# A selective state-space block with FFN on one core: half of the scan inputs made by GpSimd, and what goes with it

## Chip, core and metric

The kernel runs on one core of a Trainium2 chip. The metric is the device time of one execution in microseconds; the time given for a kernel is the median of its runs.

## The reference

x has shape (2, 1024, 512). The block is a state-space layer with a residual and a layer norm, then an FFN with a residual and a layer norm, all in float32:

```python
xn = x * rsqrt(mean(x*x) + 1e-6) * norm_w
xn = xn * sigmoid((xn @ select_proj_w.T + select_proj_b) * select_gate)
delta, B, C = split(xn @ x_proj_w.T, 128 each)
dt = softplus(delta @ dt_proj_w.T + dt_proj_b)        # (2, 1024, 512)
A = -exp(A_log)                                       # (512, 128)
h[t] = exp(dt[t] * A) * h[t-1] + (dt[t] * xn[t]) * B[t]   # h: (2, 512, 128), 1024 steps
y[t] = sum_n h[t][:, n] * C[t][n]
x = layernorm(x + (y + x * D_param) @ out_proj_w.T)
x = layernorm(x + (silu(x @ w_gate.T) * (x @ w_up.T)) @ w_down.T)   # 512 -> 2048 -> 512
```

u stands below for dt * xn. The state h has 512 channels times 128 state indices for every token, and the recurrence runs along the tokens.

## The kernel before

The 2 x 1024 tokens are cut into 64 steps of 32 tokens (S = 32, NS = 64), the steps into two halves of 256 channels, and each half into 8 groups of 32 channels: 1024 groups, counted by k in the main loop. The 128 state indices lie on the partitions. One group is one VectorE instruction, a scan over 32 channels times 32 tokens, laid end to end in the free dimension (L694). Its factors, exp(dt A), come from a_sb, and its addends, u B, from the PSUM tile bu. The factor of each channel's first token is kept at 0 so that the channels do not run into one another; what the step before carries over goes into the first addend instead (L691).

Both inputs are outer products over (state, channel x token), and TensorE makes them with matmuls of 32 rows. For the decay, the weights are 32 rows of A_log and the moving tile ddt holds dt[c, t] on the diagonal (row c, channel c) and zero elsewhere; ScalarE takes the exponential out of PSUM into a_sb (decay_mm, decay_exp, L391 and L398). For B u, the weights are 32 tokens of B and the moving tile du holds u[t, c] where row and token agree (L678). GpSimd makes ddt and du by multiplying a row that is repeated with the mask hot (function diag, L362 and L372); u and B come through DRAM, from u_d and b_d, in function load.

y_round multiplies the finished half of h by C, four tokens at a time, with the columns of cz as weights (L410). y_out takes the result from PSUM and keeps in each row only the tokens that belong to it, by the mask pick and two additions on GpSimd (L424 to L426); post adds x * D, multiplies by the output projection and normalizes. pre makes dt, u, B and C for a chunk of 256 tokens (8 steps), ffn the FFN of a chunk.

The order of all this is written out by hand. Each turn of the loop over k issues: steps of the waiting pieces on other engines (work.others), the B u matmuls of group k and the decay matmuls of group k + 1, the exponentials, the scan of group k, then the y matmuls that ROUNDS gives this turn and as many pieces of pre, post and ffn (work.tensor) as PARTS allows. Every engine runs its own instructions in that order. All transfers go through SyncE's queue. carry_a and carry_h compute what a step hands to the next; pre of a chunk must be done by the last step of the chunk before.

Of the kernel before, what the change touches and what calls it, by code (L numbers as in the profile page):

```python
# [9 lines left out]
FP = mybir.dt.float32  # L10
# [10 lines left out]
ROUNDS = ((), (0, 1, 2), (), (), (3, 4, 5), (), (), (6, 7))  # L21
PARTS = (4, 0, 3, 3, 0, 3, 3, 0)
# [3 lines left out]
V_NORM, V_SELB, V_GATE, V_DTB = range(4)  # L26

# [7 lines left out]
def kernel(  # L35
# [9 lines left out]
    sel_t: bass.AP,  # L45
    xp_t: bass.AP,
# [32 lines left out]
    u_d = dram.tile([B * L, D], FP, name="u_d")  # L79
# [15 lines left out]
    pick = const.tile([P, 4], FP, name="pick")  # L95
    nc.gpsimd.tensor_copy(pick, hot[:, 0:4])
    for g in range(1, 8):
        nc.gpsimd.tensor_tensor(pick, pick, hot[:, ts(g, 4)], ALU.add)
# [9 lines left out]
    sel_w = main.tile([P, NM, D], FP, name="sel_w")  # L108
    xp_w = main.tile([P, NM, R + 2 * N], FP, name="xp_w")
    dt_w = main.tile([P, D], FP, name="dt_w")  # L110

    a_sb = main.tile([P, 3, 32, S], FP, name="a_sb")
# [18 lines left out]
    nc.sync.dma_start(sel_w, sel_t.rearrange("(k p) e -> p k e", p=P))  # L131
    nc.sync.dma_start(xp_w, xp_t.rearrange("(k p) e -> p k e", p=P))
# [5 lines left out]
    nc.gpsimd.memset(a_sb, 0.0)  # L138
    for t in cz:
        nc.gpsimd.memset(t, 0.0)  # L140
# [23 lines left out]
    def pre(c):  # L164
# [6 lines left out]
        rms = pre_pool.tile([P, TC], FP, tag="rms", name=f"rms_{c}")  # L171
        low = pre_pool.tile([P, TC], FP, tag="low", name=f"low_{c}")
        dt = pre_pool.tile([P, NM, TC], FP, tag="dt", name=f"dt_{c}", bufs=2)
        u = pre_pool.tile([P, NM, TC], FP, tag="u", name=f"u_{c}")
        c_sb = pre_pool.tile([P, TC], FP, tag="c_sb", name=f"c_sb_{c}", bufs=2)
        made[c] = dt, c_sb
        xn = xT

        def matmuls(ps, w, m, rhs):
            for k in range(NM):  # L180
                nc.tensor.matmul(  # L181
                    ps[:, 0:TC], w[:, k, ts(m, P)], rhs[:, k, :],
                    start=(k == 0), stop=(k == NM - 1),
                )
                yield "H" if k + 1 < NM else "E"
# [30 lines left out]
        for m in range(NM):  # L216
            ps = misc(f"sel_{c}_{m}")
            yield from matmuls(ps, sel_w, m, xn)
            nc.scalar.activation(
                u[:, m, :], ps[:, 0:TC], AF.Relu,  # L220
                bias=neg[:, 1, m : m + 1], scale=neg[:, 0, m : m + 1],
            )
            nc.scalar.activation(
                dt[:, m, :], ps[:, 0:TC], AF.Abs, bias=gate_b[:, m : m + 1], scale=col(V_GATE, m)
            )
            yield "P" if m + 1 < NM else "E"
# [9 lines left out]
        for g, dst in ((0, low), (2, c_sb)):  # L236
            ps = misc(f"xp_{c}_{g}")
            yield from matmuls(ps, xp_w, g, xn)
            nc.scalar.copy(dst, ps[:, 0:TC])
            yield "P"  # L240

        ps = misc(f"b_{c}")
        for j in range(NJ):
            for k in range(NM):
                nc.tensor.matmul(  # L245
                    ps[:, ts(j, N)], xn[:, k, ts(j, P)], xp_w[:, k, R : R + N],
# [3 lines left out]
        bt = pre_pool.tile([P, NJ, N], FP, tag="bt", name=f"bt_{c}")  # L250
        nc.scalar.copy(bt, ps[:, 0:TC].rearrange("p (j n) -> p j n", j=NJ))
# [19 lines left out]

        for j in range(NJ):
            yield "P"
            ps = misc(f"uT_{c}_{j}")
            for m in range(NM):
                nc.tensor.transpose(ps[:, ts(m, P)], u[:, m, ts(j, P)], ident)
                if m == 1:
                    yield "H"
            yield "E"
            t = pre_pool.tile([P, D], FP, tag="row", name=f"uT_{c}_{j}")  # L280
            nc.scalar.copy(t, ps)
            nc.sync.dma_start(u_d[c * TC + j * P : c * TC + (j + 1) * P, :], t)
            if c == 0 and j == 0:
                load(0)
                diag(0, 0)
                diag(0, 1)
# [26 lines left out]
    prepared, carried, dus, ddts, hs, ys = {}, {}, {}, {}, {}, {}  # L313

    def load(st):


        ub = step_pool.tile([P, 2, P], FP, tag="ub", name=f"ub_{st}")
        rows = u_d[ts(st, S), :].rearrange("t (m g c) -> g t m c", g=4, c=32)
        for g in range(4):  # L320
            nc.sync.dma_start(
                ub[ts(g, S), 0, :].rearrange("t (m c) -> t m c", c=32), rows[g]
            )
            nc.sync.dma_start(ub[ts(g, S), 1, :], b_d[ts(st, S), :])
        prepared[st] = ub
# [4 lines left out]
        if st % NSB:  # L330
            cd = step_pool.tile([P, D], FP, tag="cd", name=f"cd_{st}")
            nc.sync.dma_start(cd, dt0_d[st : st + 1, :].to_broadcast([P, D]))
            carried[st] = cd

    def carry_a(st):
# [3 lines left out]
        cd = carried[st]  # L339
        nc.gpsimd.tensor_tensor(cd, a_n, cd, ALU.mult)  # L340
        nc.scalar.activation(cd, cd, AF.Exp, scale=-1.0)

    def carry_h(st, i):

        if st % NSB == 0:
            return
        cd = carried[st].rearrange("p (b i e) -> p b i e", i=2, e=16)[:, :, i, :]
        last = hs[2 * (st - 1) + i][:, :, S - 1].rearrange("p (b e) -> p b e", e=16)
        nc.gpsimd.tensor_tensor(cd, cd, last, ALU.mult)  # L349

    def diag(j, part):

        h, a = j // 2, 2 * (j % 2)
# [3 lines left out]
        name, m = divmod(part, 2)  # L357
        shape = [P, 2, 16, S]
        if name == 0:
            if m == 0:  # L360
                ddts[j] = half_pool.tile(shape, FP, tag="ddt", name=f"ddt_{j}")
            nc.gpsimd.tensor_tensor(  # L362
                ddts[j][:, m, :, :],
                made[st // SPC][0][:, a + m, toks(st)].unsqueeze(1).to_broadcast([P, 16, S]),
                hot[:, ts(i, 16)].unsqueeze(2).to_broadcast([P, 16, S]),
                ALU.mult,
            )
        else:
            if m == 0:
                dus[j] = half_pool.tile(shape, FP, tag="du", name=f"du_{j}")  # L370
            uv = prepared[st][:, 0, :].rearrange("p (m i e) -> p m i e", i=2, e=16)[:, :, i, :]
            nc.gpsimd.tensor_tensor(  # L372
                dus[j][:, m, :, :],
                uv[:, a + m, :].unsqueeze(2).to_broadcast([P, 16, S]),
                hot.unsqueeze(1).to_broadcast([P, 16, S]),
                ALU.mult,
            )
# [8 lines left out]
    def decay_mm(k, b):  # L386
# [3 lines left out]
        ps = ps_a.tile([P, 16, S], FP, tag="a", name=f"a_{k}_{b}")  # L390
        nc.tensor.matmul(  # L391
            ps, a_t[ts(g, 32), m, :], ddts[k // 4][ts(g, 32), m % 2, :, :],
            start=True, stop=True,
        )
        return ps

    def decay_exp(k, b, ps):
        nc.scalar.activation(  # L398
            a_sb[:, k % 3, ts(b, 16), 1:], ps[:, :, 1:], AF.Exp, scale=-1.0
        )  # L400
# [16 lines left out]
    def y_out(st):  # L417

        tt, s = divmod(st, 4)
        if s == 0:  # L420
            yrs[tt] = post_pool.tile([P, 4, P], FP, tag="yr", name=f"yr_{tt}")
        yc = post_pool.tile([P, P, 4], FP, tag="yc", name=f"yc_{st}")
        nc.scalar.copy(yc, ys.pop(st).rearrange("p (q t) -> p q t", t=4))  # L423
        nc.gpsimd.tensor_tensor(yc, yc, pick.unsqueeze(1).to_broadcast([P, P, 4]), ALU.mult)  # L424
        nc.gpsimd.tensor_tensor(yc[:, :, 0:2], yc[:, :, 0:2], yc[:, :, 2:4], ALU.add)
        nc.gpsimd.tensor_tensor(yrs[tt][:, s, :], yc[:, :, 0], yc[:, :, 1], ALU.add)  # L426
        if s == 3:
            work.add(post(tt), front=True)

    yrs = {}  # L430

    def post(tt):

        zT = post_pool.tile([P, NM, P], FP, tag="zT", name=f"zT_{tt}")
        nc.sync.dma_start(zT, x_q.rearrange("(m p) t -> p m t", p=P)[:, :, ts(tt, P)])
        yield "E"
        yield "E"
        nc.gpsimd.tensor_tensor(zT, zT, dq.unsqueeze(2).to_broadcast([P, NM, P]), ALU.mult)
        yield "E"
        yield "P"  # L440
        ps = misc(f"zT_{tt}")
        for s in range(4):
            nc.tensor.transpose(ps[:, ts(s, P)], yrs[tt][:, s, :], ident)
            if s == 1:
                yield "H"
        yield "E"
        z = zT.rearrange("p m (s t) -> p s m t", t=S)
        nc.vector.tensor_tensor(
            z, z, ps.rearrange("p (s m t) -> p s m t", m=NM, t=S), ALU.add
        )  # L450
# [28 lines left out]
    def ffn(c):  # L479
# [13 lines left out]
        def fetch(n):  # L493
            while len(pieces) < min(n, len(sources)):
                i = len(pieces)
                pieces.append(
                    ffn_pool.tile([P, 2 * D], FP, tag="w", name=f"w_{c}_{i}", bufs=4)
# [18 lines left out]
        for what in order:  # L516
            part = int(what[1])
            if what[0] == "g":
                hid = hid_pool[0].tile([P, NH, TC], FP, tag="hid", name=f"hid_{c}_{part}")
                hids[part] = hid, []  # L520
                for f in range(NH):
# [14 lines left out]
                    work.add(silu(gu, hid[:, f, :], f"{c}_{part}_{f}", hids[part][1]), front=True)  # L536
# [4 lines left out]
            for half in range(2):  # L541
                fetch(at + 4)
                for j in range(NJ):
                    yield "P"
                    ps = misc(f"d_{c}_{part}_{half}_{j}")
                    for f in range(NH):
                        w = pieces[at + f // 4].rearrange("p (f d) -> p f d", f=4)
# [12 lines left out]
    def silu(gu, dst, name, ready):  # L560


        e = ffn_pool.tile([P, TC], FP, tag="e", name=f"e_{name}", bufs=2)
# [4 lines left out]
        nc.scalar.activation(e, g, AF.Exp, scale=-1.0)  # L568
        nc.scalar.activation(e, e, AF.Ln, bias=ones[:, 0:1])
        yield "E"  # L570
        nc.scalar.activation(e, e, AF.Exp, scale=-1.0)  # L571
# [231 lines left out]
```

## Time and profile before

| | us |
|---|---|
| median of 3 runs | 2905.64 (2905.34 to 2907.6) |
| profiled execution, its own time | 2913.85 |
| its span, first to last instruction | 2912.1 |
| first scan starts | 64.7 |
| last scan ends, about | 2790.4 |
| 1024 scans, busy | 2340.5 |

| engine | busy us | share of the span |
|---|---|---|
| TensorE | 2751.4 | 94% |
| VectorE | 2529.0 | 87% |
| ScalarE | 1560.2 | 54% |
| GpSimd | 1783.5 | 61% |

The granted TensorE clock is 0.978 in the mean; the DMA moves 154.58 MB, 53 GB/s. In the profile PE is TensorE, PEld its weight loads, DVE VectorE, ACT ScalarE, POOL GpSimd, SPq the transfers that SyncE issues; a line in a list of groups gives the source line, the engine, output <- inputs, shapes, count, busy time and mean duration, and behind the second bar the idle time ahead of these instructions with what ended it. A float32 matmul shows as two records.

### The profile page before, as it was taken

The page shows a single profiled execution, that of the slowest core. Times are in us where ns is not written, and L with a number is a line of the kernel's source. Part 1 is how long each engine was busy: PE and PEld are TensorE (multiplying, and loading weights), DVE is VectorE, ACT ScalarE, POOL GpSimd, SP SyncE. Part 2 cuts the span into 40 slices and gives each one's busy share as a digit, 9 for nine tenths or more (in the row PEclk, how much of TensorE's full clock was granted, in tenths as well). Part 3 has the DMA queues.
Part 4 walks back from the last instruction along what each step waited for, and adds up shares of the span by engine and source line. Part 5 has one row for each costly group of instructions (what it writes and reads, how often), then busy time and mean ns, then how long its engine had stood idle before and what let it go on. Part 6 is the DMA issues. An engine that isn't in the chain of part 4 may idle for free.

```text
span 2912.1 us, 53232 instructions
## 1 busy us (share of the span) xinstructions
PE 2751.4 (94%) x20608; PEld 1383.1 (47%) x20608; DVE 2529.0 (87%) x2176; ACT 1560.2 (54%) x3073; POOL 1783.5 (61%) x2006
## 2 busy tenths in 40 slices
PE   5988789999999999999999999999999999999989
PEld 3433234444444444444544444444444444444467
DVE  0899999999899999998899999999998999999930
ACT  3554446545565455654555556555565555454533
POOL 4564556757577576665656757666675666666633
PEclk7999999999999999999999999999999999999999
DMA  2000001212112120111211221121111112111223
GB/s 82 8 19 19 19 14 57 67 45 71 55 29 63 55 70 32 54 55 50 66 32 48 65 66 55 32 75 48 59 46 56 52 55 70 44 62 60 61 82 125
DMA packets 110170, 154.58 MB, mean 53 GB/s; under 512 B 46752, under 2 KB 69792, under 8 KB 109920
## 3 DMA queue, kind: packets, MB, share of 16 engines
q1 hardware_dynamic: 109920, 151.19, 17.1%
q8 instruction: 164, 2.69, 0.4%
q14 instruction: 86, 0.70, 0.1%
HBM read 141.57 MB, written 9.57 MB: 52 GB/s over the span
## 4 chain that ended last, share of the span: by engine, by line
PE 69%; DVE 22%; issue 3%; ACT 2%; POOL 2%; DMA 1%; DVEq 0%; SPq 0%; POOLq 0%; ACTq 0%
PE bu L678 25%; DVE h L694 19%; PE gu L529 16%; PE y L410 12%; PE d L548 5%; PE a L391 4%; PE op L457 2%; PE sel L181 2%; ACT a_sb L398 1%; DVE bu L691 1%; PE xp L181 1%; PE ss L195 1%; DMA u_d<-uT 1%; PE b L245 1%; POOL du L372 0%
## 5 line engine op out<-in xcount | busy, mean ns | idle before, releaser
L694 DVE TENSOR_TENSOR_SCAN h<-a_sb,bu 128x1024 f32<-128x1024 f32 x1024 | 2340.5, 2286 | 183.3 <-PE bu L678 66.1
L398 ACT ACTIVATE a_sb<-a 128x496 f32<-128x496 f32 x2048 | 1089.5, 585 | 1064.1 <-PE a L391 945.1
L678 PE MATMUL bu<-du,ub 32*128 32x512 f32 x4096 | 1216.7, 648 | 79.5 <-DVE h L694 45.7
L391 PE MATMUL a<-ddt,a_t 32*128 32x512 f32 x4096 | 1259.3, 650 | 10.7 <-ACT t L297 8.0
L362 POOL TENSOR_TENSOR ddt<-dt,hot 128x512 f32<-128x512 f32 x512 | 533.8, 1050 | 358.7 <-PE a L391 358.7
L678 PEld LDWEIGHTS bu<-du,ub 32*128 32x128 f32 x4096 | 344.2, 185 | 484.8 <-issue 287.6
L372 POOL TENSOR_TENSOR du<-ub,hot 128x512 f32<-128x512 f32 x512 | 536.1, 1052 | 57.3 <-PE a L391 47.8
L410 PE MATMUL y<-h,cz 128*32 128x256 f32 x8192 | 533.6, 390 | 2.4 <-DVE h L694 2.4
L529 PE MATMUL gu<-x1T,w 128*128 128x256 f32 x2048 | 519.0, 395 | 4.9 <-DMA w<-in_wgu_s_dram 3.4
L529 PEld LDWEIGHTS gu<-x1T,w 128*128 128x128 f32 x2048 | 368.3, 190 | 254.1 <-issue 180.5
L410 PEld LDWEIGHTS y<-h,cz 128*32 128x32 f32 x8192 | 230.5, 111 | 418.5 <-issue 308.6
L391 PEld LDWEIGHTS a<-ddt,a_t 32*128 32x128 f32 x4096 | 379.2, 185 | 42.1 <-ACT a_sb L398 27.4
L565 POOL TENSOR_SCALAR gu<-gu 128x256 f32<-128x256 f32 x128 | 108.5, 848 | 271.1 <-ACT gu L535 270.9
L548 PE MATMUL d<-w,hid 128*128 128x256 f32 x1024 | 256.9, 394 | 10.5 <-DVE x L554 8.2
L691 DVE TENSOR_TENSOR bu<-bu,cd 128x32 f32<-128x32 f32 x992 | 184.1, 186 | 87.8 <-PE a L391 80.5
L548 PEld LDWEIGHTS d<-w,hid 128*128 128x128 f32 x1024 | 185.0, 190 | 127.5 <-issue 82.3
L424 POOL TENSOR_TENSOR yc<-yc,pick 128x512 f32<-128x512 f32 x64 | 66.6, 1041 | 146.4 <-ACT yc L423 146.4
L349 POOL TENSOR_TENSOR cd<-cd,h 128x256 f32<-128x256 f32 x124 | 106.8, 862 | 60.4 <-DVE h L694 60.3
L572 POOL TENSOR_TENSOR hid<-gu,e 128x256 f32<-128x256 f32 x128 | 93.3, 729 | 74.6 <-ACT e L571 73.9
L554 DVE TENSOR_TENSOR x<-x,d 128x256 f32<-128x256 f32 x64 | 25.6, 399 | 101.7 <-PE d L548 101.7
L535 ACT COPY gu<-gu 128x512 f32<-128x512 f32 x128 | 75.3, 588 | 67.6 <-PE gu L529 67.4
L566 POOL TENSOR_TENSOR gu<-gu 128x256 f32<-128x256 f32 x128 | 94.3, 737 | 10.7
(86 smaller groups left out, 1258.8 us busy)
## 6 DMA issues: line engine op xcount, KB each, us to landing
w<-in_wgu_s_dram SPq DMA_DIRECT2D x128, 512.0 KB, 3.7
w<-in_wd_s_dram SPq DMA_DIRECT2D x64, 512.0 KB, 3.6
cd<-dt_d SPq DMA_DIRECT2D x62, 256.0 KB, 3.7
xT<-in_x_t_dram SPq DMA_DIRECT2D x8, 512.0 KB, 4.7
u_d<-uT SPq DMA_DIRECT2D x16, 256.0 KB, 2.0
ub<-u_d SPq DMA_DIRECT2D x256, 16.0 KB, 2.0
ub<-b_d SPq DMA_DIRECT2D x256, 16.0 KB, 1.9
zT<-in_x_q_dram SPq DMA_DIRECT2D x16, 256.0 KB, 4.4
```

Of the source, the lines that this page charges most:

```text
L349: nc.gpsimd.tensor_tensor(cd, cd, last, ALU.mult)
L362: nc.gpsimd.tensor_tensor(ddts[j][:, m, :, :], made[st // SPC][0][:, a + m, toks(st)].unsqueeze(1).to_broadcast([P, 16, S]), hot[:, ts(i, ...
L372: nc.gpsimd.tensor_tensor(dus[j][:, m, :, :], uv[:, a + m, :].unsqueeze(2).to_broadcast([P, 16, S]), hot.unsqueeze(1).to_broadcast([P, 16, ...
L391: nc.tensor.matmul(ps, a_t[ts(g, 32), m, :], ddts[k // 4][ts(g, 32), m % 2, :, :], start=True, stop=True,)
L398: nc.scalar.activation(a_sb[:, k % 3, ts(b, 16), 1:], ps[:, :, 1:], AF.Exp, scale=-1.0)
L410: nc.tensor.matmul(ys[st][ts(m, 32), ts(i, 256)], cz[st % 3][:, at : at + 32], hs[h][:, ts(m, 64), ts(b, 4)], start=(i == 0 and b == 0), s ...
L529: nc.tensor.matmul(ps[:, ts(a, TC)], w[:, a, k, :], x1T[:, k, :], start=(k == 0), stop=(k == NM - 1),)
L548: nc.tensor.matmul(ps[:, 0:HD], hid[:, f, ts(j, P)], w[:, f % 4, :], start=(f == 0), stop=(f == NH - 1),)
L565: nc.gpsimd.tensor_scalar_max(g, g, -80.0)
L678: nc.tensor.matmul(bu[:, ts(b, 16), :], prepared[st][ts(g, 32), 1, :], dus[k // 4][ts(g, 32), m % 2, :, :], start=True, stop=True,)
L691: nc.vector.tensor_tensor(first, first, left[:, at : at + 2, i, :], ALU.add)
L694: nc.vector.tensor_tensor_scan(hs[h][:, ts(r, 32), :].rearrange("p q t -> p (q t)"), a_sb[:, k % 3, :, :].rearrange("p q t -> p (q t)"), b ...
```

## The change

Groups with even k (pair = 0) keep their B u by TensorE. For odd k (pair = 1), u is written to DRAM by channel (up_d), one DMA spreads a row of 32 channels x 32 tokens over all 128 partitions (load_u), and GpSimd multiplies it by B, repeated over the channels, and adds the carry to the first tokens (times_b). The scan of these groups reads that SBUF tile in place of bu. dt goes through DRAM (dt_d) and is put on the diagonals of two standing ddt tiles by 16 DMAs a half (load_decay). diag makes du alone, for the half of the channels that still needs it. The decay matmuls fill a tile of two PSUM banks, one exponential of 128x992 reads it, and a_sb has 4 places in place of 3; in a group with r4 = 0, 1, 2, 3 the exponents of 1, 2, 1, 0 later groups are issued. In even groups ScalarE copies the first addend, already summed with its carry in carry_h, into bu, in place of the VectorE addition. y_out picks rows by four matmuls with masks (pick) in place of the three GpSimd instructions. The projection weights are fetched anew for each chunk in pieces of 256 KB through two buffers (fetch_proj). w has 3 buffers, not 4, dt has 1, not 2; ROUNDS and PARTS differ.

```diff
-ROUNDS = ((), (0, 1, 2), (), (), (3, 4, 5), (), (), (6, 7))
-PARTS = (4, 0, 3, 3, 0, 3, 3, 0)
+ROUNDS = ((), (0, 1, 2), (), (), (3, 4, 5), (), (6, 7), ())
+PARTS = (3, 0, 3, 4, 0, 3, 0, 4)
...
+    def fetch_proj(n):
+        while len(projs) < min(n, 7 * NC):
+            t = pre_pool.tile([P, NM, P], FP, tag="pw", name=f"pw_{len(projs)}", bufs=2)
+            nc.sync.dma_start(t, proj_s[len(projs) % 7].rearrange("p (k e) -> p k e", k=NM))
+            projs.append(t)
...
+        nc.sync.dma_start(dt_d[:, :, ts(c, TC)], dt)
+        for m in range(NM):
+            for g in range(2, 4):
+                for i in range(2):
+                    p0 = 32 * g + 16 * i
+                    dst = up_d[ts(c, SPC), i, m, ts(g - 2, 16), :]
+                    nc.sync.dma_start(
+                        dst.rearrange("s e t -> e s t"),
+                        u[p0 : p0 + 16, m, :].rearrange("e (s t) -> e s t", t=S),
+                    )
...
+    def load_decay(h, part):
...
+        for e in range(4 * part, 4 * part + 4):
+            at = slice(16 * i + e, P, 32)
+            nc.sync.dma_start(ddt[i][at, :, e, :], dt_d[at, :, ts(st, S)])
...
+    def load_u(k):
...
+        ups[k] = half_pool.tile([P, 32, S], FP, tag="up", name=f"up_{k}", bufs=4)
+        row = up_d[st : st + 1, i, m, :, :].rearrange("s q t -> s (q t)")
+        nc.sync.dma_start(ups[k].rearrange("p q t -> p (q t)"), row.to_broadcast([P, 32 * S]))
+
+    def times_b(k):
...
+        nc.gpsimd.tensor_tensor(up, up, b.unsqueeze(1).to_broadcast([P, 32, S]), ALU.mult)
+        if st % NSB:
...
+            nc.gpsimd.tensor_tensor(first, first, left[:, at : at + 2, i, :], ALU.add)
...
+    def decay_exp(k, ps):
+        nc.scalar.activation(a_sb[:, k % 4, :, 1:], ps[:, :, 1:], AF.Exp, scale=-1.0)
...
-        nc.gpsimd.tensor_tensor(yc, yc, pick.unsqueeze(1).to_broadcast([P, P, 4]), ALU.mult)
-        nc.gpsimd.tensor_tensor(yc[:, :, 0:2], yc[:, :, 0:2], yc[:, :, 2:4], ALU.add)
-        nc.gpsimd.tensor_tensor(yrs[tt][:, s, :], yc[:, :, 0], yc[:, :, 1], ALU.add)
+        for t in range(4):
+            nc.tensor.matmul(
+                ps[:, 0:P], yc[:, :, t], pick[:, t, :], start=(t == 0), stop=(t == 3)
+            )
...
+        ahead = [j for j in ((k + 1,), (k + 1, k + 2), (k + 2,), ())[r4] if j < NG]
...
         for b in range(2):
-            g = 2 * pair + b
-            nc.tensor.matmul(
-                bu[:, ts(b, 16), :], prepared[st][ts(g, 32), 1, :],
-                dus[k // 4][ts(g, 32), m % 2, :, :],
-                start=True, stop=True,
-            )
+            if pair == 0:
+                q = r4 + b
+                nc.tensor.matmul(
+                    bu[:, ts(b, 16), :], prepared[st][1][ts(q, S), :], dus[k // 4][ts(q, S), :, :],
+                    start=True, stop=True,
+                )
+            for j in ahead:
+                decay_mm(j, b, banks[j])
...
-            nc.vector.tensor_tensor(first, first, left[:, at : at + 2, i, :], ALU.add)
+            nc.scalar.copy(
+                bu[:, :, 0].rearrange("p (g e) -> p g e", e=16),
+                first[:, r4 : r4 + 2, m // 2, i, :],
+            )
...
         nc.vector.tensor_tensor_scan(
...
-            bu.rearrange("p q t -> p (q t)"),
+            (ups.pop(k) if pair else bu).rearrange("p q t -> p (q t)"),
             0.0, ALU.mult, ALU.add,
         )
...
+        if r < 4:
+            load_decay(h + 1, r)
+        if pair:
+            load_u(k + 6)
+        else:
+            times_b(k + 3)
+        if r4 == 1:
+            diag(k // 4 + 1)
```

## The prediction

> **What bounds the kernel now.** I read the page's busy line and its chain of waits first, then the busy time by stretch, then the chain inside one half-step, then the groups of instructions by shape, and last SyncE's queue in order of time.
>
> ```profile
> PE 2751.4 (94%) x20608; PEld 1383.1 (47%) x20608; DVE 2529.0 (87%) x2176; ACT 1560.2 (54%) x3073; POOL 1783.5 (61%) x2006
> ...
> PE 69%; DVE 22%; issue 3%; ACT 2%; POOL 2%; DMA 1%; DVEq 0%; SPq 0%; POOLq 0%; ACTq 0%
> ```
>
> TensorE holds the end, with VectorE close behind. Two stretches, the first from the first scan to the last y, the second one half-step (8 groups):
>
> ```profile
> 64.74:2790.35 2725.61, 2609.79 (x19967) 1266.80 (x19964) 2518.18 (x2152) 1498.33 (x2951) 1713.45 (x1900) 0.98 0.17 50
> 1400.11:1421.25 21.14, 21.14 (x162) 10.58 (x160) 19.47 (x17) 12.30 (x25) 14.64 (x18) 1.00 0.22 75
> ```
>
> Columns: length, then busy time of PE, PEld, DVE, ACT, POOL, then clock and DMA. The stage of scans is 2725.6 us, so 21.3 us for each of 128 half-steps; 64.7 us lie before it and 121.8 us behind it. In the single half-step TensorE is never idle. The chain in it:
>
> ```profile
> 1402.50 0.62 PE bu L678
> 1403.14 0.41 PE bu L678
> 1403.57 1.00 PE y L410 x16
> 1404.57 0.62 PE bu L678
> 1405.87 1.93 PE gu L529 x8
> 1407.79 0.62 PE bu L678
> ```
>
> Each group costs TensorE one bundle of 1.07 us (1402.50 to 1403.57): B u of this group and the decay exponents of the next go side by side through it, so both together cost what one would. The rest is y and FFN pieces. The prices:
>
> ```profile
> L694 DVE TENSOR_TENSOR_SCAN h<-a_sb,bu 128x1024 f32<-128x1024 f32 x1024 | 2340.5, 2286 | 183.3 <-PE bu L678 66.1 <-PE a L391 12.1 <-ACT a_sb L398 2.8
> ...
> L372 POOL TENSOR_TENSOR du<-ub,hot 128x512 f32<-128x512 f32 x512 | 536.1, 1052 | 57.3 <-PE a L391 47.8 <-DMA ub<-u_d 7.3 <-POOL ddt L362 0.9
> L362 POOL TENSOR_TENSOR ddt<-dt,hot 128x512 f32<-128x512 f32 x512 | 533.8, 1050 | 358.7 <-PE a L391 358.7
> ...
> L691 DVE TENSOR_TENSOR bu<-bu,cd 128x32 f32<-128x32 f32 x992 | 184.1, 186 | 87.8 <-PE a L391 80.5 <-PE bu L678 6.0
> ...
> L424 POOL TENSOR_TENSOR yc<-yc,pick 128x512 f32<-128x512 f32 x64 | 66.6, 1041 | 146.4 <-ACT yc L423 146.4
> ...
> L425 POOL TENSOR_TENSOR yc<-yc 128x256 f32<-128x256 f32 x64 | 39.3, 614 | 5.0
> ...
> L209 POOL TENSOR_TENSOR xT<-xT,rms 128x512 f32<-128x512 f32 x16 | 20.3, 1271 | 14.2 <-ACT xT L204 14.2
> ```
>
> The scan reads a_sb from SBUF and bu from PSUM. Its shortest, median and longest durations are 2259, 2287 and 2291 ns while GpSimd works 63% of that stage (1713.45 of 2725.6), so the two do not disturb each other today. Every other VectorE instruction in the trace also has at most one SBUF operand.
>
> **Part by part. TensorE.** Four groups need three bundles in place of four: in the group with r4 = 3 neither B u nor exponents are issued. A half-step loses two: 21.14 - 2 x 1.07 = 19.0 us. Row picks and the extra B projection give some 0.3 us back (about 110 more pieces over the run, 0.2 to 0.5 us each by L443 and L529, over 128 half-steps): 19.3 us.
>
> **VectorE.** The add at L691 goes (992 x 0.186 = 184 us). Scans that follow each other directly start 2.23 us apart in the steps that have no such add, so 8 x 2.23 = 17.8 us, with 0.5 us of other work 18.3 us a half-step.
>
> **ScalarE.** Two exponentials of 128x496 become one of 128x992 (from the 128x256 at L568, 0.42, and the 128x512 at L341, 0.63, some 1.03 against 1.06 us, so 30 us saved over the run), and 496 copies of 128x32, at 0.2 to 0.3 each, add 100 to 150: on 1498 us of 2726 it bounds nothing. The copy is a new wait: the scan of an even group waits for it, and the next exponential is queued behind it. It is hidden by the scan of the odd group in front (2.29 us against bundle 1.07, copy 0.25, two hand-overs of 0.2). Without that cover it costs 496 x 0.45 = 220 us.
>
> **GpSimd, per half-step.** Kept work: 1713 less du 533, ddt 530 and the three yc steps 131, so 520 / 128 = 4.1 us. The du instructions halve: 2 x 1.05 = 2.1. Four products of 128x1024 with B are added. No row has this shape. By L424 and L425 (1.67 ns an element) it is 1041 + 512 x 1.67 = 1.90 us; by L209 and the 128x256 product at L566 (737 ns, so 2.09 an element) it is 2.34. The operand pattern, a tile times a row repeated over the outer dimension, is that of both L424 and L209, so I take the mean, 2.12: 8.5. Four small adds at 0.25 (L94 has that shape): 1.0. Two more adds in each carry_h at about 0.3: 0.6. Sum 16.2 us (15.3 to 17.1). [...]
>
> **The two together.** The odd scans now read a_sb and up, both from SBUF, beside GpSimd products that read SBUF too. No row shows such a scan. One bound is that nothing happens, as with the scan of today, whose second stream comes from PSUM. The other is that the two never overlap: then 4 x 2.286 = 9.1 us stand beside GpSimd's 16.2 on one line, 25.4 us a half-step (24.5 to 26.3), which is over the 19.3 of TensorE and over today's 21.3. L694 is the nearest row by operation, but what is at issue is just where it differs; my choice is the second bound, and the first is the rival. [...]
>
> GpSimd would then be busy or held all the time. Its inputs lie three groups ahead, so waits inside its queue, such as 270.9 us at L565 for ScalarE, vanish behind the backlog.
>
> **Queues.** SyncE's issues in order:
>
> ```profile
> 1428.47 0.58 SPq L324 DMA_DIRECT2D ub<-b_d  x1
> 1429.10 0.54 SPq L321 DMA_DIRECT2D ub<-u_d  x1
> ...
> 1430.39 0.36 SPq L332 DMA_DIRECT2D cd<-dt_d  x1
> ```
>
> Each holds the queue 0.4 to 0.6 us. A step gets 32 small ones for the diagonals (16 us), 8 for u (3.2), 13 for load (7), and 5 for chunk and FFN: 31 us of a step that takes 42.6 now. Bytes are no bound: 512 broadcasts of 512 KB are 268 MB, some 80 to 100 GB/s over the stage beside 50 now, while one 512 KB piece of w lands in 3.7 us. The queue fits in 51 us and nearly fills 38.6. In front of products and exponents it is hidden by three groups (7 us); if that fails, every step loses the landing, 2 us, 130 us in all. The weight streams go to the same queue: fetched one piece ahead of a 1.7 us piece and landing in about 3.7, they may hold TensorE by 0 to 2 us, 49 times, hidden where TensorE has slack, 100 us otherwise. With one buffer fewer, w still leads by a piece of 3.4 us: 0 to 5 us.
>
> **Before and behind the stage.** Streamed weights add some 3 us to the first chunk, and the first scan now waits for the new stores and 16 diagonal transfers, some 20 more issues of 0.5 us: +14 us (5 to 25). The tail keeps its FFN rest: 0, or 10 either way.
>
> **The sum.** 128 x 25.4 = 3251, + 64.7 + 14 + 121.8 = 3452 us. Changing turns costs something, 0 to 2 x 0.22 us (a usual idle time of VectorE behind TensorE) for each of 512 scans; I take 0.09 a scan, near the lower end since the next instruction is already queued: 46. So 3498 against the span of 2912.1. The profiled execution took 2913.9 us, 8.2 over the median of 2905.6; 1.8 us lie around the span. So 3498 + 1.8 - 8.2, or 3490. Bounds of this case: 24.5 and no turns, 3330; 26.3 and full turns, 3790.
>
> **The rivals.**
> *Nothing is shared.* The odd scans run as today's do. For it: every GpSimd and VectorE row of this trace. Against it: they all have one SBUF stream on VectorE. TensorE at 19.3 us bounds: 128 x 19.3 + 200 = 2670, with stalls of the filled SyncE queue up to 2900, about 2700 likely. That is faster. It decides from the point where less than a third of the 9.1 us is exclusive: 16.2 + 9.1 x 1/3 is still 19.3.
> *Shared in part.* The two interleave, and each only slows the other; a half-step between 21.3 and 24.5 us gives 2910 to 3320. For it: the scan takes an element in 2.2 ns, so half of its time its reads may leave room.
> *SyncE bounds.* Were a diagonal transfer to hold the queue 0.9 us in place of 0.5, a step would need 44 us: 64 x 44 + 200 = 3020. Against it: the median of L321 is 0.54, and the diagonal transfers have fewer rows.
>
> **Chances.** Full exclusion 0.70; shared in part or SyncE 0.07, both slower; nothing shared 0.23, of which faster 0.21 and within 0.2% 0.02. A measurement of this kernel can tell about 0.2% from no change. Slower: 0.77. The range runs from 2850, inside the upper part of the unshared case, to 3790, the upper bound of full exclusion; the likeliest case alone is 3330 to 3790.
>
> **What would show it.** Right: the odd scans stand longer than 2.29 us, or wait, and the wait leads to GpSimd; GpSimd's products exceed 2.35 us or abut the odd scans without overlap; GpSimd leads the chain of waits; TensorE's busy share falls to some 70%. Even scans stay at 2.29. Wrong: both kinds of scan at 2.29 us with products beside them, a half-step near 19 us, and TensorE still at the head of the chain. SyncE's rival would show as TensorE waiting for transfers into ddt. The picks and the copies are right if neither row heads a wait.

## The result and the profile after

The changed kernel takes 3599.27 us (median of 4 runs, 3595.14 to 3602.29) against 2905.49 (2902.18 to 2907.6) of the kernel before on the same chip: a ratio of 1.2388 (95% interval 1.2367 to 1.241). It is slower by 694 us; 3490 was forecast. The profiled execution took 3595.14 us with a span of 3593.4.

First the page of the changed kernel: the busy line, then its chain of waits by engine and by line.

```profile
PE 2890.5 (80%) x19136; PEld 1511.8 (42%) x19136; DVE 2697.1 (75%) x1232; ACT 1561.5 (43%) x2607; POOL 3148.4 (88%) x2332
...
POOL 54%; PE 17%; issue 8%; SPq 7%; DVE 6%; DMA 5%; ACT 3%; POOLq 0%; ACTq 0%; DVEq 0%
POOL up L447 21%; POOL up L452 12%; DVE h L776 6%; PE gu L602 5%; POOL du L422 4%; SPq L413 3%; DMA up<-up_d 3%; PE a L465 3%; POOL cu L404 3%; PE bu L762 3%; POOL gu L640 3%; POOL gu L639 2%; PE d L623 2%; POOL cd L399 2%; PE y L484 2%
```

GpSimd held 2% of the chain before and holds 54% now, led by the product up * B (L447) and the small addition of the carry (L452). TensorE fell from 69% of the chain to 17%, though its busy time did not fall (2751.4 us before, 2890.5 now).

The stretch from the first scan to the last (columns as in the prediction: length, busy PE, PEld, DVE, ACT, POOL, clock, DMA share, GB/s):

```profile
93.80:3470.60 3376.80, 2743.53 (x18474) 1391.42 (x18472) 2686.69 (x1208) 1502.09 (x2486) 3078.09 (x2208) 0.87 0.40 127
```

128 half-steps in 3376.8 us are 26.4 us each, where they were 21.3. GpSimd is busy for 24.0 of them. The first scan starts at 93.8 us (64.7 before), and 122.8 us follow the last (121.8 before). So the loss lies in the stage: some 650 us there, 29 ahead of it.

The page's costliest groups show by which instructions:

```profile
L776 DVE TENSOR_TENSOR_SCAN h<-a_sb,bu 128x1024 f32<-128x1024 f32 x512 | 1164.3, 2274 | 756.4 <-ACT bu L770 646.4
L776 DVE TENSOR_TENSOR_SCAN h<-a_sb,up 128x1024 f32<-128x1024 f32 x512 | 1521.2, 2971 | 12.2 <-POOL up L452 10.9
L447 POOL TENSOR_TENSOR up<-up,b_sb 128x1024 f32<-128x1024 f32 x512 | 1342.1, 2621 | 115.8 <-DMA up<-up_d 115.5
...
L452 POOL TENSOR_TENSOR up<-up,cd 128x32 f32<-128x32 f32 x496 | 686.4, 1384 | 38.9
```

The same scan takes 2274 ns with its addends in PSUM (even groups, bu) and 2971 ns with them in SBUF (odd groups, up). The odd scan is never late by the profile (12.2 us of idle time ahead of all 512): what it waits for lies inside its own duration. An addition of 32 elements a partition has a mean of 1384 ns. The spread of three lines (shortest/median/longest ns):

```profile
L776 DVE TENSOR_TENSOR_SCAN h<-a_sb,bu x512: 2252/2286/2289, 93.8 to 3466.1; 128x1024 f32<-128x1024 f32 x171
L776 DVE TENSOR_TENSOR_SCAN h<-a_sb,up x512: 2257/2820/4467, 96.0 to 3468.3; 128x1024 f32<-128x1024 f32 x171
...
L452 POOL TENSOR_TENSOR up<-up,cd x496: 263/2130/2345, 138.9 to 3459.4; 128x32 f32<-128x32 f32 x166
```

The shortest odd scan is as short as an even one (2257 ns), so it is the same work, and the longest stands 2.2 us longer, about one product. The addition's shortest is 263 ns; its median is nearly one scan. In the timeline of both engines (start, duration):

```profile
1816.06 2.26 DVE L776 TENSOR_TENSOR_SCAN h<-a_sb,up 128x1024 f32<-128x1024 f32 x1
1816.18 2.20 POOL L452 TENSOR_TENSOR up<-up,cd 128x32 f32<-128x32 f32 x1
...
1818.34 1.05 POOL L422 TENSOR_TENSOR du<-ub,hot 128x512 f32<-128x512 f32 x1
1818.85 2.29 DVE L776 TENSOR_TENSOR_SCAN h<-a_sb,bu 128x1024 f32<-128x1024 f32 x1 [0.52 <-ACT bu L770]
1819.56 2.37 POOL L447 TENSOR_TENSOR up<-up,b_sb 128x1024 f32<-128x1024 f32 x1 [0.17 <-DMA up<-up_d]
...
1821.05 3.03 DVE L776 TENSOR_TENSOR_SCAN h<-a_sb,up 128x1024 f32<-128x1024 f32 x1
...
1822.01 2.13 POOL L452 TENSOR_TENSOR up<-up,cd 128x32 f32<-128x32 f32 x1
```

The odd scan of 1816.06 ends at 1818.32, and the addition that began in it ends at 1818.38. The even scan of 1818.85 lies freely beside a product. The odd scan of 1821.05 meets that product, which ends at 1821.93; from there to the scan's end (1824.08) are 2.15 us, about the length of a scan. The addition of 1822.01 is again held to that end.

So at a turn a little of both overlaps. In the whole trace the 294 additions that begin inside an odd scan end 64 ns after it in the median, and the 469 odd scans that begin beside a GpSimd instruction end 2.147 us (median) after that one, 0.11 less than the shortest scan takes. An odd scan or a GpSimd instruction runs in 3204.2 of the stage's 3376.7 us; in 172.5 us neither does.

### The profile page after: what moved, and what is told of

The parts are those of the page before. It is cut to its first block, busy times and chain, and to the rows that moved or that the text cites. A ratio compares the mean times of both kernels' runs of the same rounds, so it can differ in the third digit from the quotient of the medians.

```text
span 3593.4 us, 52298 instructions
## 1 busy us (share of the span) xinstructions
PE 2890.5 (80%) x19136; PEld 1511.8 (42%) x19136; DVE 2697.1 (75%) x1232; ACT 1561.5 (43%) x2607; POOL 3148.4 (88%) x2332
## 4 chain that ended last, share of the span: by engine, by line
POOL 54%; PE 17%; issue 8%; SPq 7%; DVE 6%; DMA 5%; ACT 3%; POOLq 0%; ACTq 0%; DVEq 0%
POOL up L447 21%; POOL up L452 12%; DVE h L776 6%; PE gu L602 5%; POOL du L422 4%; SPq L413 3%; DMA up<-up_d 3%; PE a L465 3%; POOL cu L404 3%; PE bu L762 3%; POOL gu L640 3%; POOL gu L639 2%; PE d L623 2%; POOL cd L399 2%; PE y L484 2%
## 5 line engine op out<-in xcount | busy, mean ns | idle before, releaser
L776 DVE TENSOR_TENSOR_SCAN h<-a_sb,bu 128x1024 f32<-128x1024 f32 x512 | 1164.3, 2274 | 756.4 <-ACT bu L770 646.4
L776 DVE TENSOR_TENSOR_SCAN h<-a_sb,up 128x1024 f32<-128x1024 f32 x512 | 1521.2, 2971 | 12.2 <-POOL up L452 10.9
L447 POOL TENSOR_TENSOR up<-up,b_sb 128x1024 f32<-128x1024 f32 x512 | 1342.1, 2621 | 115.8 <-DMA up<-up_d 115.5
L465 PE MATMUL a<-ddt,a_t 32*128 32x512 f32 x4096 | 1073.4, 724 | 207.9 <-ACT a_sb L474 184.2
L474 ACT ACTIVATE a_sb<-a 128x992 f32<-128x992 f32 x1024 | 996.1, 999 | 347.7 <-PE a L465 345.2
L762 PE MATMUL bu<-du,bq 32*128 32x512 f32 x2048 | 710.9, 714 | 179.7 <-DVE h L776 163.1
L452 POOL TENSOR_TENSOR up<-up,cd 128x32 f32<-128x32 f32 x496 | 686.4, 1384 | 38.9
L762 PEld LDWEIGHTS bu<-du,bq 32*128 32x128 f32 x2048 | 195.7, 201 | 400.2 <-issue 188.8
L422 POOL TENSOR_TENSOR du<-ub,hot 128x512 f32<-128x512 f32 x256 | 293.9, 1148 | 17.1 <-DMA ub<-u_d 17.1
L639 POOL TENSOR_SCALAR gu<-gu 128x256 f32<-128x256 f32 x128 | 116.6, 911 | 115.3 <-ACT gu L608 103.3
L404 POOL TENSOR_TENSOR cu<-cu,cd 128x64 f32<-128x64 f32 x248 | 150.9, 629 | 9.8
```

The costliest lines, as they stand in the source:

```text
L404: nc.gpsimd.tensor_tensor(at, at, left[:, o, 0:2, :, i, :], ALU.add)
L422: nc.gpsimd.tensor_tensor(dus[j], prepared[st][0][:, b, i, :].unsqueeze(2).to_broadcast([P, 16, S]), hot.unsqueeze(1).to_broadcast([P, 16, ...
L447: nc.gpsimd.tensor_tensor(up, up, b.unsqueeze(1).to_broadcast([P, 32, S]), ALU.mult)
L452: nc.gpsimd.tensor_tensor(first, first, left[:, at : at + 2, i, :], ALU.add)
L465: nc.tensor.matmul(ps[:, ts(b, 16), :], a_t[ts(g, 32), m, :], ddt[h % 2][ts(g, 32), m, :, :], start=True, stop=True,)
L474: nc.scalar.activation(a_sb[:, k % 4, :, 1:], ps[:, :, 1:], AF.Exp, scale=-1.0)
```

## The experiments

The theory: a scan with both inputs in SBUF and a GpSimd instruction exclude each other, so that 4 scans and all of GpSimd's work stand on one line. The rivals: GpSimd has simply too much to do; SyncE's queue or the transfers hold it; the rest of the change (picks, diagonals, turns) costs the time. Times are medians; ratios are to the kernel before on the same chip.

### e1 and e2: where the odd scans read from

Both write bu once, at k = 0, and drop ScalarE's copies; e2 also turns the odd scans to bu. GpSimd and SyncE issue the same in both.

```diff
-        if pair == 0:            # the tile bu and its matmuls
+        if k == 0:
...
-        if pair == 0 and st % NSB:   # ScalarE's copies of first addends
+        if False:
...
-            (ups.pop(k) if pair else bu).rearrange("p q t -> p (q t)"),   # e2 only
+            bu.rearrange("p q t -> p (q t)"),
```

> The changed kernel with the B u matmuls and the copies of the first addends left out: bu is written once, at the first group, and all even groups scan this stale tile; odd groups scan up from SBUF as before. It is the partner of the next run. Theory, exclusion: GpSimd's work (17.2 us a half-step by the shortest or median durations of the changed kernel's rows) and the four odd scans (4 x 2.275 = 9.1) take turns, 26.3 us a half-step, so 128 x 26.3 and 217 around the stage, 3400 to 3600 us, and odd scans last 2.8 to 3.1 us in the mean. Rival, SyncE's queue or the transfers bound: the same 3500 to 3600, but then the next run is the same too. Rival, the waits for the copies bound (VectorE waits 646 us for ScalarE's copies): they are gone here, so 2900 to 3000.

> As the run before it, but odd groups also scan the stale bu in PSUM instead of up: same transfers, same GpSimd instructions, no scan with two SBUF inputs, and no scan that waits for a product. Theory, exclusion: nothing is shared any more, GpSimd's small adds fall from 1.38 to 0.26 us, its sum from 24 to 17.2 us a half-step, and TensorE, GpSimd or SyncE bounds at 19 to 20 us: 2600 to 2850 us. Rival, SyncE's queue or the transfers bound: over 3400 us. Rival, GpSimd is slow by itself beside any scan: its adds stay at 1.4 us and the time over 3200.

Measured: e1 3571.34 us, 1.2301 (1.2276 to 1.2326); e2 2986.66 us, 1.0287 (1.0261 to 1.0314). Three groups of e1, then the stage and the same groups of e2:

```profile
L776 DVE TENSOR_TENSOR_SCAN h<-a_sb,up 128x1024 f32<-128x1024 f32 x512 | 1459.8, 2851 | 432.1 <-POOL up L452 129.3
L447 POOL TENSOR_TENSOR up<-up,b_sb 128x1024 f32<-128x1024 f32 x512 | 1371.4, 2679 | 92.8 <-DMA up<-up_d 91.6
...
L452 POOL TENSOR_TENSOR up<-up,cd 128x32 f32<-128x32 f32 x496 | 529.4, 1067 | 38.9
```

```profile
93.62:2856.90 2763.28, 2492.52 (x16430) 1291.77 (x16428) 2327.53 (x1208) 1444.45 (x1990) 2203.76 (x2208) 0.92 0.48 155
```

```profile
L776 DVE TENSOR_TENSOR_SCAN h<-a_sb,bu 128x1024 f32<-128x1024 f32 x1024 | 2272.7, 2270 | 418.1 <-ACT a_sb L474 312.6
L447 POOL TENSOR_TENSOR up<-up,b_sb 128x1024 f32<-128x1024 f32 x512 | 1209.5, 2362 | 295.2 <-DMA up<-up_d 294.8
...
L452 POOL TENSOR_TENSOR up<-up,cd 128x32 f32<-128x32 f32 x496 | 134.0, 270 | 38.9
```

With one operand moved to PSUM 585 us go. The held GpSimd rows fall to their own price: the addition from 1067 to 270 ns (1384 in the changed kernel), the product from 2679 to 2362 (2621). The same products read and write the same SBUF in both runs, so neither their number nor the transfers made the time. e2 drops one thing more: its odd scans no longer depend on the product and the addition that write up. That dependence cannot be the bulk of it: in the changed kernel the odd scans stand idle for 12.2 us in all, and e10 below keeps the dependence, takes only the reading out of the products, and falls by 317 us against e9. Removing matmuls and copies while the odd scans still read SBUF (e1) brought 28 us; the 646.4 us that the changed kernel's even scans wait for ScalarE's copy therefore lie almost wholly in GpSimd's shadow.

e2 prices the line: GpSimd unheld works 2203.8 us in the stage, 17.2 a half-step; with 4 odd scans of 2.27 us that makes 26.3, and 26.4 was measured. (In e1 it was 26.2, so the sum holds to a few tenths of a microsecond and no closer.)

e2 also missed its own band of 2600 to 2850: with nothing held a half-step still takes 21.6 us, not TensorE's 19.3. TensorE's busy time there is 19.5, near the forecast although B u is left out, but 2.1 us of waits stay.

### e9: the small addition out

```diff
-        if st % NSB:
+        if False:
```

> The changed kernel with the small adds on up left out, so the odd groups do not get their carry. They take 686 us in the profile, 1.38 us each, but 0.26 at the shortest. Theory, exclusion: the rest of their time is waiting for an odd scan, which the next GpSimd instruction then waits out; the sum of a half-step falls by 4 x 0.26 from 26.4 to 25.4, so 3430 to 3490 us, and the products' mean duration rises from 2.62 towards 3.5 us. Rival, the adds are slow by themselves: 686 us less, about 2910.

Measured: 3518.72 us, 1.2109 (1.2073 to 1.2144); 80 us gone of the line's 686, and the time lies 29 us above the expected band. The products' mean duration rose only to 2741 ns, not towards 3500. Two groups that took the addition's place:

```profile
L422 POOL TENSOR_TENSOR du<-ub,hot 128x512 f32<-128x512 f32 x256 | 455.8, 1781 | 18.5 <-DMA ub<-u_d 17.4
...
L646 POOL TENSOR_TENSOR hid<-gu 128x256 f32<-128x256 f32 x128 | 242.1, 1891 | 37.8 <-ACT gu L645 37.7
```

du had 1148 ns, hid 740 in the changed kernel. The addition's 1384 ns are a place in the queue, not a price: what comes next meets the odd scan instead. Its own work, 134 us by e2, is what leaves the line; 80 came out at the end. The half-step fell by 0.6 us (26.4 to 25.8) where the sum fell by 1.05, and waits grew beside it (for the transfers of up from 115.5 to 157.9 us, among others).

### e10: products that only write

```diff
-        nc.gpsimd.tensor_tensor(up, up, b..., ALU.mult)
-        if st % NSB:
+        nc.gpsimd.memset(up, 0.001)
+        nc.gpsimd.memset(up, 0.001)
+        nc.gpsimd.memset(up[:, 0:16, :], 0.001)
+        if False:
```

> As the run before it, but each product is replaced by three memsets of the same tile, some 2.3 us together, which write SBUF and read nothing. Theory, exclusion of reads alone: what must take turns is the rest of GpSimd's work, 6.8 us, and the odd scans, 9.1, so no longer the bound, and the half-step goes to 21 to 22 us as in the run with all scans from PSUM: 2930 to 3080 us. If writes are excluded too, the time stays at 3400 to 3490.

Measured: 3201.62 us, 1.1017 (1.0985 to 1.105), between the bands of the two theories. The trace is plainer than the time. First one line's spread, then the timeline of both engines:

```profile
L447 POOL MEMSET up<- x512: 941/951/977, 94.2 to 3066.1; 128x1024 f32 x171
```

```profile
1803.54 1.05 POOL L422 TENSOR_TENSOR du<-ub,hot 128x512 f32<-128x512 f32 x1
1803.95 2.78 DVE L778 TENSOR_TENSOR_SCAN h<-a_sb,up 128x1024 f32<-128x1024 f32 x1
1804.53 0.95 POOL L447 MEMSET up<- 128x1024 f32 x1
1805.54 0.95 POOL L448 MEMSET up<- 128x1024 f32 x1
...
1810.26 2.27 DVE L778 TENSOR_TENSOR_SCAN h<-a_sb,up 128x1024 f32<-128x1024 f32 x1
...
1811.01 1.59 POOL L549 TENSOR_SCALAR off_a<-mv_a,rstd_a 128x1 f32<-128x1 f32 x1 [1.29 <-ACT rstd_a L668]
```

The memsets lie inside the odd scan at their usual length: those of 1804.53 and 1805.54 take 0.95 us each beside the scan of 1803.95, and none of the 512 of L447 exceeds 977 ns. The scan of 1803.95 is 0.5 us longer than its usual 2.27; du, which reads SBUF, still had 0.64 us to go when it began. At 1811.01 an instruction that reads 128x1 elements is held to the scan's end, 1812.5; its 1.59 us were 0.27 in the kernel before (L474, mean). So beside these odd scans the GpSimd instructions that read SBUF were held, and the memsets, which only write, were not. The three memsets take 2.43 us together, about as long as a product by itself, so the 317 us against e9 go with the reading alone. What keeps this run at 3200 is not settled: its chain is shared by TensorE (36%) and GpSimd (27%), and its scans still wait 586.9 us for the copies.

### e12: the product on VectorE

Nothing is left out; the product moves to VectorE.

```diff
-        nc.gpsimd.tensor_tensor(up, up, b..., ALU.mult)
+        nc.vector.tensor_tensor(up, up, b..., ALU.mult)
```

> The changed kernel with the products of u and B on VectorE in place of GpSimd; nothing is left out. By the 128x512 additions of VectorE, 0.66 us, a product of 1024 should take about 1.2. Theory, exclusion: GpSimd keeps 7.8 us, odd scans 9.1, products 4.8, so 21.7 us that take turns, and VectorE itself 18.3 + 4.8 = 23.1 us a half-step is the bound: 3130 to 3300 us, between the two kernels. Rival, SyncE, the transfers or the copies bound the changed kernel: 3500 and more, as VectorE only gets more work.

Measured: 3795.37 us, 1.3061 (1.3023 to 1.3098), a plain miss: the slowest of all. The product itself became cheap (median 1200 ns on VectorE). The addition that follows it did not:

```profile
L452 POOL TENSOR_TENSOR up<-up,cd 128x32 f32<-128x32 f32 x496 | 886.6, 1788 | 1540.9 <-DVE up L447 1501.1
```

This addition now waits for VectorE's product (1501.1 us in all), with GpSimd's other work queued behind it in the order of the program; and VectorE goes from the product straight into the odd scan, which holds the addition again (1788 ns, unheld 270). The expectation had summed the work of each engine and priced no hand-over between them.

### e3: half of SyncE's queue out

The 16 diagonal transfers of a half run only for the first two halves.

```diff
-        if h >= 2 * NS:
+        if h >= 2:
```

> The changed kernel with the transfers that put dt on the diagonals left out after the first step: 2016 of 2048 small transfers go, ddt keeps old values. They are half of what SyncE's queue issues. Theory, exclusion: GpSimd's 290 us of idle time in the stage shrink at most, 3400 to 3590 us. Rival, SyncE's queue bounds: it falls from some 31 to 15 us a step's issue time, so below 3100.

Measured: 3556.2 us, 1.2249 (1.2224 to 1.2273), 43 us less. SyncE as the bound falls. In the changed kernel's trace one of these transfers holds the queue as long as was assumed:

```profile
L413 SPq DMA_DIRECT2D ddt<-dt_d x2048: 499/500/896, 79.7 to 3424.8; - x187
```

### e4 to e8: parts of the change without the GpSimd groups

Starting from the kernel before (weights stay as they were): e5 puts dt on diagonals by DMA; e8 takes the new ROUNDS and PARTS; e6 takes these and the picks by TensorE; e7 lays yc out so that the weights of a pick are contiguous; e4 is e5 and e6 together.

```diff
-        yc = post_pool.tile([P, P, 4], FP, tag="yc", name=f"yc_{st}")
-        nc.scalar.copy(yc, ys.pop(st).rearrange("p (q t) -> p q t", t=4))
+        yc = post_pool.tile([P, 4, P], FP, tag="yc", name=f"yc_{st}")
+        nc.scalar.copy(yc, ys.pop(st).rearrange("p (q t) -> p t q", t=4))
...
-                ps[:, 0:P], yc[:, :, t], pick[:, t, :], start=(t == 0), stop=(t == 3)
+                ps[:, 0:P], yc[:, t, :], pick[:, t, :], start=(t == 0), stop=(t == 3)
```

(e7 against e6)

> The kernel before with two other parts of the change: dt on the diagonals by DMA in place of GpSimd, and rows of y picked by TensorE, with the ROUNDS and PARTS of the change. All B u stays on TensorE, no scan has two SBUF inputs, and the projection weights are not streamed. Theory, exclusion: TensorE still bounds at 21.3 us a half-step and some 0.3 more for the picks, GpSimd falls below 10: 2880 to 3000 us. Rival, the small transfers and the queue cost the time: over 3200.

> The kernel before with one part of the change: dt goes through DRAM and is put on the diagonals by 16 small transfers a half-step; GpSimd's 512 ddt instructions go. The run with this part and the row picks took 2994 us, 90 over the kernel before. Theory: that came from the picks, and this part costs nothing on TensorE: 2870 to 2920 us, and less than before if TensorE's waits for GpSimd (34 us for du, 20 for ddt) go. Rival: the small transfers come late and cost the 90 us: 2980 to 3010.

> The kernel before with the rows of y picked by TensorE, with the ROUNDS and PARTS of the change; the ddt tiles stay GpSimd's. Theory: 64 picks of four matmuls take 2.06 to 2.13 us each on a TensorE that has nothing to spare, 134 us, less some 20 for the transposes that go: 2980 to 3020 us. Rival, the small transfers cost the 90 us of the run with both: 2900 to 2925.

> As the run before it, but ScalarE's copy of y turns (q, t) into (t, q), so that the weights of each pick lie side by side and not every fourth element. Theory: the weight loads of 327 ns, against 140 to 190 ns for 128x128 weights that lie side by side, set the 2.1 us of a pick; it falls to 1.0 to 1.2 us, so 60 to 70 us less than the run before it: 2915 to 2960 us. Rival: the four pairs of matmuls take their 0.4 us each anyway: within 10 us of the run before it.

> The kernel before with nothing but the ROUNDS and PARTS of the change: a control for the two runs before it, which carry them. TensorE issues the same work in another order: 2890 to 2925 us by the theory; a rival that the order itself costs the 90 us gives 2980 or more.

| | us | ratio (95%) |
|---|---|---|
| e8: ROUNDS and PARTS | 2918.1 | 1.0053 (1.0037 to 1.0069) |
| e5: dt by DMA | 2929.09 | 1.0092 (1.0074 to 1.011) |
| e6: e8 and the picks | 2974.1 | 1.0248 (1.0221 to 1.0275) |
| e7: e6, contiguous weights | 2942.63 | 1.0138 (1.0116 to 1.0161) |
| e4: e5 and e6 | 2994.49 | 1.0312 (1.0295 to 1.0329) |

Each part loses a little; e5 lies 9 us above its expected band, e6 6 us below its own. The picks are the dearest (56 us over e8). The groups of e6, then of e7:

```profile
L435 PE MATMUL zT<-pick,yc 128*128 128x128 f32 x512 | 136.6, 410 | 8.0 <-ACT yc L424 4.6 <-DVE bu L693 1.3 <-DVE x L556 1.1
L435 PEld LDWEIGHTS zT<-pick,yc 128*128 128x128 f32 x512 | 124.3, 327 | 57.5 <-issue 29.2 <-ACT yc L424 22.1 <-DVE x L556 3.4
```

```profile
L435 PE MATMUL zT<-pick,yc 128*128 128x128 f32 x512 | 74.1, 288 | 8.0 <-ACT yc L424 4.6 <-DVE bu L693 1.3 <-DVE x L556 1.1
L435 PEld LDWEIGHTS zT<-pick,yc 128*128 128x128 f32 x512 | 62.0, 191 | 57.5 <-issue 30.7 <-ACT yc L424 20.5 <-DVE x L556 3.4
```

Weights taken as every fourth element load in 327 ns, contiguous ones in 191; the matmuls' busy time falls by 62.5 us and the run by 31, half of the 60 to 70 expected. Of e5's loss of 28 us, 12 are start-up: its first scan is at 77.1 us. The rest was not taken apart.

### e11: e2 with contiguous picks and without diagonal transfers

Its edits are those of e2, e3 and e7 on the changed kernel.

> The run with all scans from PSUM (2987 us) with two more things taken away: the small diagonal transfers after the first step, and the strided weights of the picks (ScalarE's copy turned). Nothing is shared. It asks what the half-step of 21.6 us there was made of, where the forecast had 19.3. If picks and SyncE's queue made it: 2780 to 2900 us. If it is TensorE, ScalarE and VectorE waiting on each other in turn: 2920 to 2970.

Measured: 2885.28 us, 0.993 (0.9905 to 0.9956). Picks and diagonals account for 101 of e2's 2987 us. Still a half-step takes 20.8 us, not 19.3: with no exclusion at all, without B u by TensorE and without copies, it ends only 0.7% below the kernel before. It leaves work out, so it shows how far this plan could get at best and is no version to use.

No run that computes everything was faster than the kernel before. An addend in PSUM for the odd scans, made without TensorE, was not tried.

## Why the prediction was right, and where its sizes were off

**The mechanism was the one forecast.** Full exclusion was to give a half-step of 25.4 us of work, with turns 25.8; 26.4 was measured. No row of the kernel before shows a scan with two SBUF inputs: that it and GpSimd's work never overlap was the author's choice between two bounds, and by e2's unheld work and the changed kernel's trace the two overlap by only some 0.3 us a scan (155 us, below). The signs of the mechanism came: odd scans of 2971 ns beside even ones of 2274, products of 2621 ns, GpSimd at the head of the chain. Two others did not: TensorE's share is 80% and not some 70, and ScalarE's copies do head the even scans' waits (both below). e1 against e2, with e10, shows the cause: the place of one operand and 585 us, then the reading alone and 317. (The stretch that the prediction calls "to the last y" ends with the last scan, at 2790.35 us; the sum is not touched by that.)

**The product was mis-sized.** The term "I take the mean, 2.12" is the largest error. Unheld it takes 2362 ns (e2), the pattern of L209 (the upper bound, 2.34), not that of L424. At 512 products that is 0.24 x 512 = 123 us too little, and the whole list of GpSimd came out at 17.2 where 16.2 was summed.

**The turns were over-sized, and not of that kind.** "0.09 a scan, 46 us" has no counterpart: at a turn the two engines overlap. GpSimd's own 2203.8 us (e2) and 512 odd scans of 2.257 us, the shortest, make 3359 us, but one or the other runs in only 3204: 155 us of overlap, some 0.3 a scan. Against it stand the 172.5 us in which neither runs, which the prediction put at nothing. What is left, 17 us, is small because these two nearly cancel; that the sum of both engines comes so close to the time is in part luck. The stage's 80 us are thus 108 too little of work (3359 against 3251) less 29 too much for turns (46 against 17), but for rounding.

**The start was mis-sized.** "+14 us (5 to 25)" measured 29.1. e5 puts 12 of it on dt and its diagonals, e4 19 on dt, picks and order; the other 10 belong to the parts e4 lacks, the stores and spreads of u and the streamed weights among them; they were not taken apart.

**The sum again with measured terms:** 128 x 26.38 = 3377, + 93.8 + 122.8 = 3593, the span. The forecast span was 3498: 80 short in the stage, 15 in the start, 1 in the tail.

**The rivals.** *Nothing shared* is rejected by e1 and e2; it was also priced too low: its "about 2700" took TensorE's 19.3 us as the half-step, and e2 needs 21.6, e11 20.8. So the chance of 0.21 for faster rested in part on a price that was out of reach, since even unshared the change would have ended near the kernel before, on its slow side by e2. *Shared in part* falls by the timeline and the sum: 26.4 is all of both, but for the 0.3 us of overlap at each scan. *SyncE bounds* falls by e3 and by 500 ns a transfer where 0.9 us was the point of decision.

**The picks.** "0.2 to 0.5 us each" came from pieces with one weight load and was too low: a pick is four loads with strided weights, 2.06 us in e4's timeline. In the changed kernel this lies beside GpSimd's line.

**TensorE.** Its share fell to 80%, not 70: its busy time in the stage is 21.4 us a half-step and not 19.3, at a granted clock of 0.87 where it was 0.98 (decay matmuls 724 ns, before 650). In e2, at 0.92, the same plan without B u took 19.5. TensorE's part in the changed kernel's chain is 17%.

**Copies and waits.** "Hidden by the scan of the odd group in front" did not hold as put: in 267 cases the even scan waits for the copy. The end did not move with it (e1, 28 us). "Waits vanish behind the backlog" held in part: 103.3 us of 270.9 stay for ScalarE in the FFN, and 115.5 for the transfers of up are new.

## What to carry to other kernels

Before work moves to GpSimd, count the SBUF inputs of what VectorE runs beside it. With two, as in the odd scans here, the GpSimd instructions that read SBUF stood in one line with the scan (an addition of 270 ns in e2 took 1384 in the mean), and since that line was the longest, the sum of both, 26.3 us a half-step, was about the time, 26.4. With the second input in PSUM (e2) the same instructions overlapped freely: no addition took more than 320 ns, no product more than 2407. The wait showed here in no list of waits (12.2 us ahead of all 512 odd scans), only as a duration (2971 ns against 2274): compare the shortest instance of a group with its median, and the same operation by the place of its operands. The tiny instruction with the big mean, 1384 ns, was a place in the queue; taking it out moved the hold to the next ones (e9: du from 1148 to 1781 ns, hid from 740 to 1891).

## What the runs showed of the hardware that was not expected

- A GpSimd addition of 128x32 elements that takes 263 ns at its shortest was held to the odd scan's end, 2130 ns in the median (the changed kernel); an instruction of 128x1 was held as well (1.59 us in e10, 0.27 in the kernel before).
- GpSimd's memsets of 128x1024 were not held while an odd scan ran (L447 of e10: 941 to 977 ns).
- A turn overlapped instead of costing: a held addition, 270 ns by itself (e2), ended 64 ns after the scan (median), and a held scan, 2.257 us at its shortest, ended 2.147 us after the GpSimd instruction.
- The granted clock of TensorE fell from 0.978 to 0.869 in a kernel that keeps TensorE busy for less of its span (80% against 94%); why was not studied.
- Weights of 128x128 with a stride of four elements loaded in 327 ns (e6), contiguous ones in 191 (e7).
